# Four-layer convolution block, last image: the variance of the residual sum from a covariance, and the residual sums inside the q, k, v loop

## The chip, the cores and the metric

The kernel runs on one core of a Trainium2 chip, in float32. The metric is the device time of one execution in microseconds (us). Before the change it is 3103.75 us, the median of 3 runs (3103.21 to 3104.64). Stretches of the profile are given in us from the start of its span.

The engines: TensorE (PE; weight loads PEld) for matrix products, VectorE (DVE), ScalarE (ACT), GpSimd (POOL), and SyncE (SP), which issues most of the DMA transfers. Each runs its own instructions in their written order.

## The reference, cut to what matters

Four images of 256 channels and 64 x 64 pixels pass through four residual layers. Layer 0 is a convolution with group norm and a non-local attention over the 4096 pixels, layer 1 a linear attention, layer 2 a convolution with generated kernels, layer 3 a mixture of experts. Ahead of each layer stands a group norm. The change lies between layer 0 and layer 1:

```python
    # layer 0, its end
    attn = jax.nn.softmax(f, axis=-1)
    y = jnp.einsum('bnm,bmc->bnc', attn, g_x)
    ...
    w_y = group_norm(conv1x1(y, w_w, w_b), gn2_w, gn2_b)
    return w_y * 0.1 + xs
    ...
    x = x + _L0_conv_ref(_gn(x), ...)
    x = x + _L1_conv_ref(_gn(x), ...)    # layer 1: rmsnorm, q, k, v, context, out, rmsnorm
```

So layer 1 needs the group mean and variance of r + s * wy, where r is the residual (x plus the convolution's result, kept in `xs_d`), wy the attention's output after its 1 x 1 convolution, and s a scale per channel which is known only when the statistics of wy over the whole image are.

## The kernel before

The 256 channels are two halves (`h`) of 128 partitions; 4096 pixels are eight blocks (`q` or `c`) of 512 columns. The order of instructions on every engine is the order in which the Python code emits them. `Chain` (L47) is a generator with a rate, so that the tail of one image can be emitted in between the attention of the next.

**Attention.** `attend(b)` (L888) has eight blocks `q` of 16 iterations `m`. An iteration emits the logits of the next step (two products `pf`, two exponentials into a probability tile `pr`), four products `py`, and one addition into `tot` on VectorE. After each block, `ended` (L902) runs in four steps, one in each of the following iterations: sum `inv`, product `pss`, reciprocal, `yt`, the products `ps_wy` into `wt`, then `bn_stats` of `wt`, and the store of `wt` to `wy_d`. The wide working tiles (`pr`, `tot`, `wt`, `xg`, `sq`, `qk`, `v1`, `dw`, `wy`, ...) come from one pool, `k4` (L106), of nine buffers of 128 x 1024.

**Images.** While attention of image 3 (the last) runs, the tail of image 2 is emitted beside it (L1590). It ends with the load of the residual of image 3 into `x_cols` (L1546), and it leaves 16 products of its last layer in the list `held`. `fill(n)` puts n of these into places where TensorE would be idle, `settle` emits their additions (`res`) and stores. When the tail of image 2 is done, attention runs alone, and `residual_sums` (L956) is emitted beside it: 16 copies on ScalarE with an accumulator, for the mean of r.

**The tail of the last image.** `nonlocal_out` (L966) issues six loads of wy parts of 128 x 1024, waits for the end of the attention, and calls `group_finish` (L330) on the statistics of wy: aggregate, mean over a group by a product `pm`, variance by a product `pv`, `rstd` by a power on GpSimd (`rsqrt`, L215). `affine` gives scale `sc` and shift `sh`. Then come eight sums into `big` (for this image: `tpg`) of 128 x 1024 on VectorE (L1009, recorded as L127), each followed by a square with an accumulator on ScalarE (L1014); their total is the variance.

`linear_attention` (L1023) calls `group_finish` again, on that mean and variance. The loop over eight blocks `c` follows: `normed` (L1029) makes `xg` and its square `sq` on ScalarE and adds the halves into `s2` on VectorE; `qkv` (L1049) multiplies by `wqkv_s` (16 matmuls, `ps_qkv`), with the row norms by `norms` (L1040: product `ps_ss`, `rinv` on VectorE, a power on GpSimd), the exponentials of q and k (L1061) and the copy of v (L1062) on ScalarE; `context` (L1072) transposes q and accumulates the context. `normed(c + 1)` is emitted ahead of `qkv(c)`. For the last image the working tiles alternate between `k4` and four spare buffers (`in_turns`, L1561).

Of the kernel before, what the change touches and what calls it, by code (L numbers as in the profile page):

```python
# [93 lines left out]
def conv_preact_fast(ctx: ExitStack, tc: tile.TileContext, guard, x, wc, wtpg, ww, wqkv, wout, w1cat, wd2,  # L94
# [235 lines left out]
    def group_finish(st, avg, eps, shift=None):  # L330


        if callable(st):
            mv = st()
        else:
            mv = sp.tile([P, NH, 2], F32, name="mv")
            for h in range(NH):
                nc.vector.bn_aggr(mv[:, h, :], st[:, h, :, :].rearrange("p c s -> p (c s)"))
        if shift is not None:
            tt(mv[:, :, 0], mv[:, :, 0], shift, ALU.add)  # L340
        yield 1
        pm = bank("pm")
        nc.tensor.matmul(pm[:, 0:NH], avg, mv[:, :, 0], start=True, stop=True)
        gm = sp.tile([P, NH], F32, name="gm")
        nc.vector.tensor_copy(gm, pm[:, 0:NH])
        ev = sp.tile([P, NH], F32, name="ev")
        tt(ev, mv[:, :, 0], gm, ALU.subtract)
        tt(ev, ev, ev, ALU.mult)
        tt(ev, ev, mv[:, :, 1], ALU.add)
        yield 1  # L350
        pv = bank("pv")
        nc.tensor.matmul(pv[:, 0:NH], avg, ev, start=True, stop=True)
        rstd = sp.tile([P, NH], F32, name="rstd")
        nc.vector.tensor_scalar(rstd, pv[:, 0:NH], eps, None, ALU.add)  # L354
        rsqrt(rstd, rstd)
        return mv, gm, rstd
# [530 lines left out]

    def attend(b):  # L888

        probs, todo = {}, []  # L890
        st = wy_stats[b] = sp.tile([P, NH, 8, 6], F32, name="wy_st")

        def logits(i):
            q, m = divmod(i, NM)
            pr = k4("pr")
            for s in range(2):
                pf = bank("pf")
                nc.tensor.matmul(pf, phi[:, bass.ts(2 * m + s, P)], theta[:, bass.ts(q, 512)], start=True, stop=True)  # L898
                nc.scalar.activation(pr[:, bass.ts(s, 512)], pf, AF.Exp)  # L899
            probs[i] = pr  # L900

        def ended(q, py, tot):  # L902

            at = b * NQ + q
            inv = wk.tile([P, 512], F32, tag="inv", name="inv")
            nc.vector.scalar_tensor_tensor(inv, tot[:, 0:512], 1.0, tot[:, 512:CH], ALU.mult, ALU.add,
                                           accum_out=guard[:, 0, at:at + 1])
            yield
            pss = bank("pss")
            nc.tensor.matmul(pss, ones, inv, start=True, stop=True)  # L910
            yield
            nc.vector.reciprocal(inv, pss)  # L912
            yt = k2("yt")
            tt(yt, py, inv, ALU.mult)
            yield
            nc.scalar.activation(junk(), inv, AF.Copy, accum_out=guard[:, 1, at:at + 1])

            wt = k4("wt").rearrange("p (h n) -> p h n", h=NH)
            for h in range(NH):
                ps = bank("ps_wy")  # L920
                nc.tensor.matmul(ps, ww_s[:, bass.ts(h, P)], yt, start=True, stop=True)  # L921
                nc.scalar.copy(wt[:, h, :], ps)
            yield
            for h in range(NH):
                nc.vector.bn_stats(st[:, h, q, :], wt[:, h, :])
            nc.sync.dma_start(out=wy_d[b].rearrange("h p n -> p h n")[:, :, bass.ts(q, 512)], in_=wt)

        logits(0)
        for i in range(NQ * NM):
            q, m = divmod(i, NM)  # L930
            if m == 0:
                py = bank("py")
                tot = k4("tot")
            if i + 1 < NQ * NM:
                logits(i + 1)
            for s in range(2):
                nc.tensor.matmul(py, g[:, bass.ts(2 * m + s, P)], probs[i][:, bass.ts(s, 512)],  # L937
                                 start=(m == 0 and s == 0), stop=(m == NM - 1 and s == 1))
            if m == 1:
                tt(tot, probs[i - 1], probs[i], ALU.add)  # L940
            elif m > 1:
                tt(tot, tot, probs[i], ALU.add)
            for t in todo:
                next(t, None)
            if m == NM - 1:
                todo = [ended(q, py, tot)]
                next(todo[0])
            yield i + 1 < NQ * NM
        for t in todo:
            for _ in t:  # L950
                yield


    res_sum = cp.tile([P, NH], F32, name="res_sum")

    def residual_sums(xs_in):  # L956

        parts = sp.tile([P, NH, N // 512], F32, name="res_parts", bufs=1)
        for h in range(NH):
            for c in range(N // 512):  # L960
                nc.scalar.activation(junk(), xs_in[:, h, bass.ts(c, 512)], AF.Copy, accum_out=parts[:, h, c:c + 1])
                yield
        nc.vector.tensor_reduce(res_sum, parts, AX.X, ALU.add)


    def nonlocal_out(w, b, big, k4, xs_in):  # L966
# [4 lines left out]
        def load_parts(i):  # L971
            c, h = PARTS[i]
            wy = k4("wy")
# [7 lines left out]
        ahead = 2 if xs_in is None else 6  # L981
        parts = [load_parts(i) for i in range(ahead)]
        if xs_in is not None:
            yield 1
        bias = vec_s[:, V_WB, :]
        wmv, gm, rstd = yield from group_finish(wy_stats[b], avg32, 1e-5, bias)
        sc, sh = affine(gm, rstd, vec_s[:, V_G2W, :], vec_s[:, V_G2B, :], bias, 0.1)
        st = stats_tile()
        if xs_in is not None:

            mv = sp.tile([P, NH, 2], F32, name="mv_in", bufs=1)
            centre = sp.tile([P, NH], F32, name="centre", bufs=1)
            squares = sp.tile([P, NH, N // CH], F32, name="squares", bufs=1)
            tt(mv[:, :, 0], wmv[:, :, 0], bias, ALU.subtract)
            tt(mv[:, :, 0], mv[:, :, 0], sc, ALU.mult)
            stt(mv[:, :, 0], res_sum, 1.0 / N, mv[:, :, 0], ALU.mult, ALU.add)
            nc.vector.tensor_scalar(centre, mv[:, :, 0], -1.0, None, ALU.mult)

            def moments():
                nc.vector.tensor_reduce(mv[:, :, 1], squares, AX.X, ALU.add)  # L1000
                nc.vector.tensor_scalar(mv[:, :, 1], mv[:, :, 1], 1.0 / N, None, ALU.mult)
                return mv

            st = moments
        w.fill(2)
        for i, (c, h) in enumerate(PARTS):
            cols = bass.ts(c, CH)
            wy, xs = parts[i]
            stt(big[:, h, cols], wy, sc[:, h:h + 1], xs, ALU.mult, ALU.add)  # L1009
            if i + ahead < len(PARTS):  # L1010
                parts.append(load_parts(i + ahead))
            yield 0.6
            if xs_in is not None:
                nc.scalar.activation(wy, big[:, h, cols], AF.Square, bias=centre[:, h:h + 1], accum_out=squares[:, h, c:c + 1])  # L1014
            else:
                for s in range(2):
                    nc.vector.bn_stats(st[:, h, 2 * c + s, :], big[:, h, bass.ts(2 * c + s, 512)])
            yield 0.6
        w.settle()
        return st, sh  # L1020


    def linear_attention(w, b, big, qT, k4, st, sh, alone):  # L1023
        _, gm, rstd = yield from group_finish(st, avg8, 1e-5, sh)
# [56 lines left out]

        ahead = normed(0)
        yield 1
        ready = *ahead, None
        last = None
        for c in range(NC):
            if c + 1 < NC:
                ahead = normed(c + 1)
            yield 0.5
# [9 lines left out]
        rk = sp.tile([P, 1], F32, name="rk")  # L1099
# [98 lines left out]
    def generated(w, b, big, k4, st, sh, diag):  # L1198
        mv, gm, rstd = yield from group_finish(st, avg8, 1e-5, sh)

        pivot = sp.tile([P, NH], F32, name="pivot")
# [7 lines left out]
        hs = sp.tile([HT * HP, NC3], F32, name="hs")  # L1209
# [6 lines left out]
        b1n = sp.tile([HT * HP, 1], F32, name="b1n")  # L1216
# [33 lines left out]
        pooled = sp.tile([HT * HP, 1], F32, name="pooled")  # L1250
        nc.vector.tensor_reduce(pooled, hs, AX.X, ALU.add)
        pd = sp.tile([HT * HP, 2 * R], F32, name="pd")
# [5 lines left out]
        pb = sp.tile([P, 2 * R], F32, name="pb")  # L1258
# [3 lines left out]
        dk = sp.tile([P, NH * 9], F32, name="dk")  # L1262
# [177 lines left out]
    def mixed(w, b, big, k4, st, sh, held):  # L1440
# [7 lines left out]
        pool = sp.tile([P, NH], F32, name="rpool")  # L1448
# [6 lines left out]
        hid = sp.tile([EH, 1], F32, name="hid")  # L1455
# [6 lines left out]
        nm = sp.tile([P, 1], F32, name="lnm")  # L1462
        nc.vector.tensor_reduce(nm, pl[:, 0:NE], AX.X, ALU.max, negate=True)
        al = sp.tile([P, NE], F32, name="al")
        asum = sp.tile([P, 1], F32, name="asum")
# [5 lines left out]
        scales = sp.tile([P, NH, NE], F32, name="scales")  # L1471
# [15 lines left out]
        b3 = sp.tile([P, NH], F32, name="b3")  # L1487
# [46 lines left out]
    def tail(b, big, qT, k4=k4, diag=None, xs_in=None, held=None):  # L1534

        def layers(w):
            st, sh = yield from nonlocal_out(w, b, big, k4, xs_in)
            st = yield from linear_attention(w, b, big, qT, k4, st, sh, diag is not None)
# [33 lines left out]
    with tc.manual_schedule(engines={E.PE, E.Activation, E.DVE, E.Pool, E.SP}):  # L1572
# [20 lines left out]
        sums = residual_sums(x_cols)  # L1593
        while next(attention, False):
            for _ in range(3):
                next(sums, None)
        for _ in sums:
            pass
# [592 lines left out]
```

## Time and profile before

| what | us |
|---|---|
| median of 3 runs | 3103.75 |
| the profiled execution itself | 3104.24 |
| its span, first to last instruction | 3102.5 |
| attention of the last image, with the tail of image 2 beside it | about 2244 to 2820 |
| end of attention to the first `xg` of the last image's q, k, v loop | 2820.7 to 2848.73 |
| q, k, v loop of the last image, to the last context product | 2849.59 to 2914.5 |
| end of the span | 3102.5 |
| DMA: one load of 512 KB from `wy_d`, median from issue to landing | 4.7 |
| DMA: one load of 512 KB from `xs_d`, the same | 5.4 |

How to read it: a row of the timeline is start, duration, engine, line, operation, output and inputs; in brackets the idle time of its engine ahead of it, and what ended that. Many operations are issued by helpers, so L124 is any `tensor_tensor`, L127 any `scalar_tensor_tensor`, and L217 any power on GpSimd; the tile's name tells which. An accumulating operation is recorded as two, the second (`READ_ACCUMULATOR`) reading the accumulator. The chain of waits is followed back from the last instruction; what released a step is inferred. The granted clock is TensorE's, as a share of full speed. An operation's record is a little longer than its pitch: the eight sums take 1.28 us each, and start 1.195 us apart.

### The profile page before, as it was taken

To read this page: it belongs to the slowest core of one execution; us is meant where nothing else is said; L and a number is where in the kernel's file an instruction comes from. 1 tells how busy PE (TensorE), PEld (TensorE's weight loads), DVE (VectorE), ACT (ScalarE), POOL (GpSimd) and SP (SyncE) were. 2 spreads that over 40 slices of the span, in tenths; PEclk is the share of its full clock that TensorE was granted. 3 is DMA by queue.
4 is the path that set the end of the run, shared out by engine and by line. 5 is a ranking of instruction groups with operands and counts; after the bars stand their busy time and mean duration, and the time that the engine had idled before them with its cause. 6 is when DMAs were issued, how large, how long until landed. Compare 5 with 4: busy or idle time off the path is not lost.

```text
span 3102.5 us, 24417 instructions
## 1 busy us (share of the span) xinstructions
PE 3005.3 (97%) x8606; PEld 1486.3 (48%) x8606; DVE 2108.8 (68%) x2713; ACT 1173.3 (38%) x2188; POOL 131.0 (4%) x178
## 2 busy tenths in 40 slices
PE   6899999999999999999999999999999999998998
PEld 3354555445554444444565444444546544444643
DVE  8747777853557986787536897778363668865485
ACT  2134333353555332323364532222445443335621
POOL 0100000000010000000011000000000100000100
PEclk9999999999999999999999999999999999998999
DMA  5233111122100023113300102311420010021021
GB/s 218 79 100 140 34 48 31 34 51 79 51 11 30 12 75 126 38 38 65 115 8 4 34 27 75 115 41 34 95 82 1 11 34 7 16 80 68 8 68 66
DMA packets 58913, 174.25 MB, mean 56 GB/s; under 512 B 6432, under 2 KB 16416, under 8 KB 54560
## 3 DMA queue, kind: packets, MB, share of 16 engines
q1 hardware_dynamic: 54752, 155.85, 14.6%
q0 software_dynamic: 4032, 16.78, 2.9%
q8 instruction: 70, 1.15, 0.2%
q14 instruction: 59, 0.48, 0.1%
HBM read 111.26 MB, written 78.12 MB: 61 GB/s over the span
## 4 chain that ended last, share of the span: by engine, by line
PE 77%; DVE 16%; issue 5%; ACT 1%; DMA 0%; POOL 0%; POOLq 0%; ACTq 0%; DVEq 0%; SPq 0%
PE pf L898 22%; PE py L937 22%; PE ps_qkv L1057 5%; PE ps_conv L499 4%; PE ps_tp L874 4%; DVE dw L127 4%; PE ps_ex L1498 3%; DVE tot L124 3%; PE ps_pw L1298 3%; PE ps_conv L571 2%; PE ps_g L879 2%; PE ps_wy L921 2%; PE ps_o L1125 1%; PE ps_dw L1343 1%; DVE big L127 1%
## 5 line engine op out<-in xcount | busy, mean ns | idle before, releaser
L899 ACT ACTIVATE pr<-pf 128x512 f32<-128x512 f32 x1024 | 603.1, 596 | 1184.5 <-PE pf L898 1138.8
L898 PE MATMUL pf<-tpg 128*128 128x512 f32 x2048 | 969.3, 596 | 2.9 <-ACT pr L899 2.9
L937 PE MATMUL py<-pr,tpg 128*128 128x512 f32 x2048 | 962.3, 592 | 2.5 <-ACT pr L899 2.3
L124 DVE TENSOR_TENSOR tot<-tot,pr 128x1024 f32<-128x1024 f32 x448 | 546.0, 1219 | 181.1 <-ACT pr L899 179.7
L937 PEld LDWEIGHTS py<-pr,tpg 128*128 128x128 f32 x2048 | 388.8, 190 | 494.8 <-issue 476.1
L898 PEld LDWEIGHTS pf<-tpg 128*128 128x128 f32 x2048 | 381.9, 190 | 438.1 <-issue 412.5
L127 DVE SCALAR_TENSOR_TENSOR dw<-xp,dk,dw 128x1008 f32<-128x1008 f32 x208 | 262.9, 1267 | 9.9 <-ACT dw L1290 7.0
L499 PE MATMUL ps_conv<-v,u 128*128 128x512 f32 x384 | 171.0, 593 | 3.6 <-DVE v L124 3.6
L1057 PE MATMUL ps_qkv<-wqkv_s,xg 128*128 128x384 f32 x384 | 129.9, 487 | 0.0
L124 DVE TENSOR_TENSOR tpg<-ps_g,bg_s 128x512 f32<-128x512 f32 x32 | 22.1, 691 | 145.7 <-PE ps_g L879 145.7
L874 PE MATMUL ps_tp<-big,wtpg_s 128*128 128x512 f32 x256 | 118.1, 605 | 3.0 <-ACT big L671 3.0
L499 PEld LDWEIGHTS ps_conv<-v,u 128*128 128x128 f32 x384 | 72.6, 190 | 96.4 <-issue 89.8
L217 POOL TENSOR_TENSOR rstd<-rstd,half 128x2 f32<-128x2 f32 x24 | 16.8, 699 | 2359.6 <-DVE rstd L354 2227.4
L912 DVE RECIPROCAL inv<-pss 128x512 f32<-128x512 f32 x32 | 107.2, 3351 | 7.1 <-PE pss L910 7.1
L1298 PE MATMUL ps_pw<-dw,pk 128*128 128x512 f32 x224 | 101.3, 592 | 0.0
L1057 PEld LDWEIGHTS ps_qkv<-wqkv_s,xg 128*128 128x128 f32 x384 | 72.2, 190 | 53.5 <-issue 9.3
L1067 DVE TENSOR_REDUCE qs<-qk 128x16 f32<-128x512 f32 x24 | 16.5, 686 | 118.6 <-ACT qk L1061 118.6
L875 ACT ACTIVATE tpg<-ps_tp,btp_s 128x512 f32<-128x512 f32 x64 | 43.8, 686 | 119.7 <-PE ps_tp L874 119.7
L874 PEld LDWEIGHTS ps_tp<-big,wtpg_s 128*128 128x128 f32 x256 | 47.9, 195 | 55.0 <-issue 50.6
L1127 ACT ACTIVATE junk<-ps_o 128x256 f32<-128x256 f32 x128 | 49.1, 384 | 63.7 <-PE ps_o L1125 59.4
L1061 ACT ACTIVATE qk<-ps_qkv,rinv 128x256 f32<-128x256 f32 x96 | 45.5, 473 | 72.5 <-PE ps_qkv L1057 61.8
L124 DVE TENSOR_TENSOR v<-ra 128x1024 f32<-128x1024 f32 x58 | 69.5, 1219 | 0.4
(338 smaller groups left out, 3123.8 us busy)
## 6 DMA issues: line engine op xcount, KB each, us to landing
xp<-in_x_dram SPq DMA_DIRECT2D x16, 1024.0 KB, 6.5
wy_d<-wt SPq DMA_DIRECT2D x32, 512.0 KB, 3.0
out_dram<-res SPq DMA_DIRECT2D x64, 256.0 KB, 2.0
wy<-wy_d SPq DMA_DIRECT2D x28, 512.0 KB, 4.7
xs_d<-big POOLq DMA_DIRECT2D x24, 512.0 KB, 11.1
u<-filters SPq DMA_DIRECT2D x48, 256.0 KB, 2.5
xs<-xs_d SPq DMA_DIRECT2D x24, 512.0 KB, 5.4
u<-rows_d SPq DMA_DIRECT2D x36, 256.0 KB, 3.1
```

The source lines that it names most:

```text
L124: nc.vector.tensor_tensor(o, a, b, op)
L127: nc.vector.scalar_tensor_tensor(o, a, s, b, op0, op1)
L499: nc.tensor.matmul(ps[oh], u(oh, h), v[:, bass.ts(h, 512)], start=(h == 0), stop=(h == NH - 1))
L571: nc.tensor.matmul(ps[:, bass.ts(oh, IY * IX)], u[i][:, h, bass.ts(oh, P)], v[:, i, bass.ts(h, IY * IX)], start=(h == 0), stop=(h == NH - 1))
L874: nc.tensor.matmul(ps, wtpg_s[:, h, k, :], big[:, h, cols], start=(h == 0), stop=(h == NH - 1))
L898: nc.tensor.matmul(pf, phi[:, bass.ts(2 * m + s, P)], theta[:, bass.ts(q, 512)], start=True, stop=True)
L899: nc.scalar.activation(pr[:, bass.ts(s, 512)], pf, AF.Exp)
L912: nc.vector.reciprocal(inv, pss)
L937: nc.tensor.matmul(py, g[:, bass.ts(2 * m + s, P)], probs[i][:, bass.ts(s, 512)], start=(m == 0 and s == 0), stop=(m == NM - 1 and s == 1))
L1057: nc.tensor.matmul(ps[:, 0:3 * HID], xg[:, h, bass.ts(j, P)], wqkv_s[:, h, :], start=(h == 0), stop=(h == NH - 1))
L1298: nc.tensor.matmul(ps, pk[:, h * NH * P + oh * P:h * NH * P + (oh + 1) * P], dw[h][:, bass.ts(s, 512)], start=(h == 0), stop=(h == NH - 1))
L1498: nc.tensor.matmul(ps, wm[h][:, bass.ts(oh, P)], big[:, h, bass.ts(c, 512)], start=(h == 0), stop=(h == NH - 1))
```

## The change

It concerns the last image alone (and some small tiles, which now have one buffer in place of two).

1. In the last attention, a tile `xc` of `k4` is loaded from `xs_d` in every block, at m = 9: the block of r that belongs to the block of wy. At m = 12 and 14, `bn_stats` of its halves go to `res_st`. When the block's `wt` is there, `with_residual` multiplies (wy - pivot) by r with an accumulator (`joint`), one instruction for each half. The pivot is the mean of wy over the first block. The two multiplies of the last block are kept in `last_block`, and are emitted inside the first `group_finish` of the tail.
2. `residual_sums` and the squares are gone. Mean and variance of the sum follow from those of r and wy and from the covariance, by small operations of 128 x 2.
3. The eight sums are emitted by a generator, `on_the_way`: the first half-chunk of both halves inside the second `group_finish`, the rest inside the q, k, v loop, about a chunk ahead of `normed`.
4. The tail's wy parts come from `k4` alone, four loads ahead and two more at a time in the loop; before it were six, alternating between `k4` and the spare buffers.
5. One of the two held products filled in ahead of the sums is now filled in after the second `group_finish`; their additions are emitted there too, ahead of the loop.

```diff
-    def group_finish(st, avg, eps, shift=None):
+    def group_finish(st, avg, eps, shift=None, between=()):
...
         tt(ev, ev, mv[:, :, 1], ALU.add)
+        for f in between[0:1]:
+            f()
         yield 1
...
         rsqrt(rstd, rstd)
+        for f in between[1:]:
+            f()
...
+        def multiply(q, h, wt, xc):
+            nc.vector.scalar_tensor_tensor(xc[:, h, :], wt[:, h, :], pivot_in[:, h:h + 1], xc[:, h, :], ALU.add, ALU.mult,
+                                           accum_out=joint[:, h, q:q + 1])
+
+        def with_residual(q, wt, xc):
+
+            if q == 0:
+                mv = sp.tile([P, NH, 2], F32, name="mv")
+                for h in range(NH):
+                    nc.vector.bn_aggr(mv[:, h, :], st[:, h, 0, :])
+                nc.vector.tensor_scalar(pivot_in, mv[:, :, 0], -1.0, None, ALU.mult)
+            if q < NQ - 1:
+                for h in range(NH):
+                    multiply(q, h, wt, xc)
+            else:
+                last_block.extend(lambda h=h: multiply(q, h, wt, xc) for h in range(NH))
...
+            if b == B - 1:
+                with_residual(q, wt, xc)
...
+            if b == B - 1 and m == 9:
+                xc = k4("xc").rearrange("p (h n) -> p h n", h=NH)
+                nc.sync.dma_start(out=xc, in_=xs_d[b].rearrange("h p n -> p h n")[:, :, bass.ts(q, 512)])
+            if b == B - 1 and m in (12, 14):
+                h = m // 2 - 6
+                nc.vector.bn_stats(res_st[:, h, q, :], xc[:, h, :])
...
-            wy = k4("wy")
+            wy = (k4 if xs_in is None else pool4)("wy")
...
-        ahead = 2 if xs_in is None else 6
-        parts = [load_parts(i) for i in range(ahead)]
+        parts = [load_parts(i) for i in range(2 if xs_in is None else 4)]
...
+            tt(mv[:, :, 0], wmv[:, :, 0], bias, ALU.subtract)
+            tt(off, mv[:, :, 0], pivot_in, ALU.add)
+            for h in range(NH):
+                nc.vector.bn_aggr(rmv[:, h, :], res_st[:, h, :, :].rearrange("p c s -> p (c s)"))
+            nc.vector.tensor_reduce(cov, joint, AX.X, ALU.add)
+            tt(off, off, rmv[:, :, 0], ALU.mult)
+            stt(cov, cov, 1.0 / N, off, ALU.mult, ALU.subtract)
         sc, sh = affine(gm, rstd, vec_s[:, V_G2W, :], vec_s[:, V_G2B, :], bias, 0.1)
...
+            w.fill(1)
             tt(mv[:, :, 0], mv[:, :, 0], sc, ALU.mult)
...
+            tt(mv[:, :, 0], mv[:, :, 0], rmv[:, :, 0], ALU.add)
+            tt(mv[:, :, 1], wmv[:, :, 1], sc, ALU.mult)
+            stt(mv[:, :, 1], cov, 2.0, mv[:, :, 1], ALU.mult, ALU.add)
+            tt(mv[:, :, 1], mv[:, :, 1], sc, ALU.mult)
+            tt(mv[:, :, 1], mv[:, :, 1], rmv[:, :, 1], ALU.add)
+
+            def on_the_way():
+
+
+                for s in range(2):
+                    for h in range(NH):
+                        cols = bass.ts(s, 512)
+                        wy, xs = parts[h]
+                        stt(big[:, h, cols], wy[:, cols], sc[:, h:h + 1], xs[:, cols], ALU.mult, ALU.add)
+                        if s == 0:
+                            yield
+                yield
+                for c in range(1, N // CH):
+                    if c > 1:
+                        parts.extend(load_parts(2 * c + h) for h in range(NH))
+                        yield
+                    for h in range(NH):
+                        added(2 * c + h, sc)
+                    yield
+
+            return (lambda: mv), sh, on_the_way()
...
+        _, gm, rstd = yield from group_finish(st, avg8, 1e-5, sh, (lambda: next(sums),) * 2 if alone else ())
         nb = norm_bias(gm, rstd, sh)
...
+        if alone:
+            w.fill(1)
+        w.settle()
         ahead = normed(0)
+        if alone:
+            next(sums)
         yield 1
...
                 ahead = normed(c + 1)
+            if alone:
+                next(sums, None)
             yield 0.5
             this = yield from qkv(*ready)
```

## The prediction, made before the changed kernel was run

> **What bounds the kernel now.** I read the page first: one engine carries the span, and the clock falls at one place only.
>
> ```profile
> PE 3005.3 (97%) x8606; PEld 1486.3 (48%) x8606; DVE 2108.8 (68%) x2713; ACT 1173.3 (38%) x2188; POOL 131.0 (4%) x178
> ...
> PE   6899999999999999999999999999999999998998
> ...
> PEclk9999999999999999999999999999999999998999
> ```
>
> TensorE is full except at the start and in slice 37 (2792 to 2870 us), where the granted clock dips too. That slice holds the hand-over from the last attention to the tail of the last image. Next, the chain of work that ended last, for 2740 to 3103:
>
> ```profile
> 2828.41 2.75 DMA wy_d<-wt
> 2831.22 3.90 DMA rt<-wy_d
> 2835.15 8.45 DVE tpg L127 x7
> 2843.60 1.32 DVE res L127 x2
> 2845.39 0.60 PE pm L343 x2
> ...
> 2847.77 0.68 POOL rstd L217
> 2848.47 0.17 DVE nb L124
> 2848.73 0.82 ACT ra L1033
> 2849.59 2.93 PE ps_qkv L1057 x4
> 2852.52 1.50 PE ps_ss L1043 x8
> 2854.02 6.51 PE ps_qkv L1057 x12
> 2860.53 0.79 PE ps_ss L1043 x8
> 2861.32 5.27 PE ps_qkv L1057 x16
> ```
>
> The two DMA lines are an inference: the transfer happened to land at 2835.12, just as the second residual sum started behind the first. What holds the tail is the eight sums on VectorE with the squares on ScalarE behind them: the group statistics cannot start before all eight. From the third `ev` of the first statistics (end 2831.02) to the first `xg` (2848.73) it is 17.7 us, and TensorE has 0.7 us or less in each 2 us window between 2836 and 2848. Third, the windows, 2 us each (after the range: the length, then PE, PEld, DVE, ACT, POOL, and the granted clock):
>
> ```profile
> 2838.00:2840.00 2.00, 0.00 (x0) 0.00 (x0) 2.00 (x3) 2.00 (x4) 0.00 (x0) 1.00 0.00 0
> 2842.00:2844.00 2.00, 0.00 (x0) 0.00 (x0) 2.00 (x3) 2.00 (x5) 0.00 (x0) 0.50 0.00 0
> 2856.00:2858.00 2.00, 2.00 (x5) 1.09 (x4) 0.00 (x0) 1.21 (x4) 0.00 (x0) 0.50 0.00 0
> ```
>
> The clock halves in the gap and stays halved until about 2859, so the first chunk of q, k, v costs 11.73 us from 2849.59 to 2861.32, where a later chunk has 5.16 + 0.79 = 5.95. From 2868.76 each chunk is 7.34 us of TensorE without a gap.
>
> Call T the start of the first `xg` on ScalarE. Before: T = 2848.73, and the third chunk's products start at 2868.76 = T + 20.03. The path through the change is these two lengths.
>
> **Part 1, the statistics.** Removed from the path: eight sums at 1.195 us pitch (2833.95 to 2843.5), the last square (to 2844.9), two `res` additions standing between, two small operations. In their place, from 2831.02:
> - First `multiply` of the last block, between `ev` and `rstd`. Nearest row: the accumulating sum at L906, 0.69 us, next instruction 0.74 after its start. The matrix product it hides behind allowed `rstd` at 2831.50; now 2831.80, +0.3.
> - Second `multiply`, 0.74: to about 2832.6. Before, the power was done and `sc` started at 2832.56, so this costs nearly nothing.
> - Covariance: two aggregates at 0.31 and five small operations, dependent ones 0.19 apart: 1.3, to 2833.9. All of it stands ahead of `sc` in VectorE's order.
> - `affine`, six operations as now, 0.73 (2832.56 to 2833.29): to 2834.65.
> - Variance by formula, six operations and the shift, about 1.05: the shift starts at 2835.7.
> - From the shift to the first `xg` it was 2845.18 to 2848.73, 3.55. The first half-chunk sum (0.61) now stands between `ev` and `rstd`, where 0.84 passes anyway waiting for the product `pv`: nothing. The second stands beside the power on GpSimd.
>
> Here a rule speaks against the change. The trace has GpSimd powers beside a VectorE addition with both inputs in SBUF:
>
> ```profile
> 2432.21 0.17 DVE L1132 TENSOR_SCALAR zr<-zr 128x4 f32<-128x4 f32 x1 [1.81 <-ACT junk L1127]
> 2432.28 1.22 DVE L124 TENSOR_TENSOR tot<-tot,pr 128x1024 f32<-128x1024 f32 x1
> 2432.46 1.91 POOL L217 TENSOR_TENSOR zr<-zr,half 128x4 f32<-128x4 f32 x1 [8.50 <-DVE zr L1132]
> ```
>
> 1.91 us, where the median of this power is 1.008. The Trainium skill, "SBUF — State Buffer", section "Who interferes with whom", explains it: such a VectorE instruction and a GpSimd instruction that reads SBUF exclude each other for the whole instruction. The change puts one beside both `rstd` powers. The first is covered by covariance work. For the second: the sum ends 0.73 after `rstd` starts, the power needs about 0.55 more, 1.28 in place of the 1.03 measured (2847.44 to 2848.47): +0.25. Without the rule 0. I take 0.25, as the row agrees.
>
> So T after = 2835.7 + 3.55 + 0.25 = 2839.5, a gain of 9.2 (bounds 8.4 and 9.7, from a fifth either way on the roughly 3 us of small operations, and from the lock).
>
> **Part 2, the sums inside the q, k, v loop.** They don't vanish: 9.6 us of VectorE now run in the loop. After T: `s2` of chunk 0 comes at T + 2.64, as before (two `xg`, then the square), and ends T + 3.33. Its two remaining half-chunk sums end T + 4.6. ScalarE's `xg` of chunk 1 waits for them: T + 4.1 to 5.6, square to T + 6.7, `s2` to T + 7.4. Then two full sums, 2.4, to T + 9.8. Only behind them in VectorE's order stands the `rinv` of chunk 0; the exponentials wait for it: from `rinv` to `exp` is 1.28 (2854.47 to 2855.75), so T + 11.1, where it was T + 7.02. That is 4.1 late, and it is what is late next. Following on: four exponential pairs 2.6, `xg` and square of chunk 2 2.6, `s2` 0.7 (T + 17.0), norms 0.8, transposes and context 1.4: the third chunk starts at T + 19.3, against T + 20.03 now. The delay is absorbed because before, TensorE at half clock took those 19 us itself. It has done chunk 1 by about T + 16, or T + 17.9 if the clock stays halved until T + 9, which makes T + 20.1. Bounds: T + 18.5 and T + 21.5; I take 19.3, gain 0.7.
>
> A rule on the clock bears on that. The rows show half clock up to 9 us after the products began. The Trainium skill, "TensorE: Matmul & The Clock Gate", "Part 1: The HAM clock gate", has full clock after about 3.4 us of sustained work. One held product (four matmuls) is moved to stand just ahead of the loop, so by the rule full clock comes near T + 2 to T + 5; by the rows, which I follow for the bound, near T + 8. The sum is 19.3 by the one and 20.1 by the other. The product itself delays the first q, k, v product by 0.9 at half clock, covered by the wait for `s2`.
>
> From the third chunk on, ScalarE has about 6 of 7.34 us to do and VectorE 2.5, plus 2.4 in every second chunk: covered by TensorE, 0. Uncovered it would be 2.4 a time. Loads 4 to 7 are issued one chunk (7.3 us) ahead, against 4.7 to land: 0.
>
> **Part 3, the last attention.** Added: eight loads of 512 KB on SyncE's queue, 16 statistics at 0.61 pitch, 14 multiplies at 0.74, three small operations: 21 us of VectorE between 2244 and 2820. VectorE is idle for about 205 of the 580 us from 2240 to 2820, and TensorE waits for nothing there: the list of TensorE's waits is empty. It is tightest here:
>
> ```profile
> 2540.00:2560.00 20.00, 20.00 (x48) 8.89 (x47) 19.82 (x20) 6.68 (x12) 0.00 (x0) 1.00 0.18 52
> ```
>
> A lump of 1.3 us lands in it. What TensorE needs from VectorE then, `inv`, ends at 2560.6 and `pss` starts 2565.9: 5.3 spare. The pointwise products at 2592.5 follow the last tap by 1.9, and VectorE idles 0.8 and 0.9 shortly before. Queued behind a statistic that waits for its load are the `tot` additions, which free the probability buffers. The load has three iterations of 3.43 = 10.3 us against 5.4 to land (the page's `xs` loads). On SyncE the store of `wt` and the tail's loads queue behind it, as they now do behind stores.
>
> The unknown is the buffer: `xc` holds one of nine of `k4` for 10 of 16 iterations. The trace doesn't show how many are spare. No gain is possible, TensorE having no gap; removing 16 ScalarE copies with their accumulator reads (12.3 us) gains nothing for the same reason. Upper end: one exponential, 0.6, uncovered in each of some 37 holding iterations of the tap stage: 22. Nearest row: TensorE's empty wait list. I take 0.5. The `bufs=1` edits cost nothing: their tiles are used once an image.
>
> **Sum.** Against the profiled execution's own time, 3104.24 (span 3102.5 and 1.74 around it): 3104.24 - 9.2 - 0.7 + 0.5 = 3094.84. The median of the runs is 0.49 below that execution, so 3094.4.
>
> **Rivals.** (a) The loop gives it back: the exponentials' 4.1 us are not absorbed, because TensorE would have been warm anyway. 3103.75 - 9.2 + 4.1 + 0.5 = 3099.2. For it: `rinv` stands behind two full sums. Against: the 11.73 us of the first chunk. (b) Slower: `xc` starves the probability ring. At 22 us, 3103.75 - 9.9 + 22 = 3115.9; it decides above 9.9 / 37 = 0.27 us per holding iteration. For it: nine buffers shared by attention, taps and filters, with VectorE at 19.8 of 20. Against: VectorE catches up within 15 us, and TensorE never waited. (c) The change doesn't free the path because the first sums wait for reloads: all four early loads now take `k4` buffers. Three such loads were issued by 2805.3; even one issued at 2820 lands by 2825, twelve us before need. A late one costs 2 to 5: 3096 to 3099.
>
> **Chances.** Forecast 0.74; (a) 0.12; (b) 0.07, most of it slower; (c) 0.07. Measurement tells about 0.2% (6.2 us) from no change, so faster means below 3097.5. Of (c), and of milder forms of (a), a little counts as faster: 0.79 faster, 0.15 within, 0.06 slower. Range 3091.0, by the good ends of parts 1 and 2, to 3100.0, which takes in (a).
>
> **What would show it.** Right: in the changed trace no squares at L1014; the first `xg` 8.4 to 9.7 us earlier after the attention's last `inv`; the first exponential about 11 after `xg`; the third chunk about 19 after it; both `rstd` powers above 0.70; the attention's length unchanged within 1 us. Wrong: TensorE waits before 2820, or the third chunk beyond T + 21.5.

## The result and the profile after

The changed kernel takes 3094.76 us (median of 9 runs, 3093.55 to 3097.48) against 3103.75: ratio 0.9972, 95% interval 0.9963 to 0.9981. The forecast was 3094.4. Its profiled execution spans 3093.0 us, 9.5 less than the 3102.5 before. The number is close; the terms behind it are less so: one part came out 3.2 us worse than forecast, and what made up for it, 3.3 us in all, was in good part luck.

The page of the changed kernel, the same lines as before:

```profile
PE 3002.1 (97%) x8606; PEld 1485.2 (48%) x8606; DVE 2130.3 (69%) x2772; ACT 1153.3 (37%) x2140; POOL 131.8 (4%) x178
...
PE   6899999999999999999999999999999999998998
...
PEclk9999999999999999999999999999999999999999
```

VectorE has 21.5 us more to do, ScalarE 20 us less, TensorE the same matmuls: the gain is no saved work. The chain of waits, from the second statistics into the loop:

```profile
2836.45 0.16 DVE ev L124
2836.61 0.51 DVE tpg L127
2837.13 0.07 issue
2837.19 0.16 DVE rstd L357
...
2837.52 1.05 POOL rstd L217
...
2838.79 1.53 ACT ra L1088 x2
...
2846.15 2.39 DVE tpg L127 x2
2848.54 0.08 DVE rinv L1100
...
2854.85 0.70 DVE s L124
2855.55 0.14 issue
2855.69 1.84 PE ps_ss L1098 x8
2857.52 0.95 PE ps_qt L1131 x4
2858.48 1.72 PE ps_ctx L1134 x8
2860.20 6.35 PE ps_qkv L1112 x16
2866.55 0.79 PE ps_ss L1098 x8
```

The eight sums and the two DMA lines are gone from in front of the first `xg` (here `ra L1088`, 2838.79). Two sums (2846.15) now stand in the chain ahead of `rinv`. The last lines hold what the forecast lacked: the norms `ps_ss` take 1.84 and then, four lines on, 0.79 for the same eight matmuls. The windows (columns as in the prediction) show why, and a row of the timeline has the wait ahead of it:

```profile
2854.00:2856.00 2.00, 0.31 (x2) 0.34 (x2) 0.69 (x1) 1.82 (x5) 1.01 (x2) 0.91 0.00 0
2856.00:2858.00 2.00, 2.00 (x11) 2.00 (x11) 0.63 (x1) 1.59 (x6) 0.00 (x0) 0.50 0.62 152
2862.00:2864.00 2.00, 2.00 (x7) 1.20 (x6) 2.00 (x3) 0.73 (x2) 0.00 (x0) 0.88 0.00 0
```

```profile
2855.69 1.84 PE L1098 MATMUL ps_ss<-ones,s 128*128 128x1 f32 x8 [2.43 <-DVE s L124]
```

TensorE had finished the second chunk (`c` = 1) at 2853.26 and waited 2.43 us for the third chunk's `s2`; then its clock was halved until 2862.5.

The table gives the stages of every profiled run, counted from the start of the attention's last product `pss`, since the attention itself ends up to 1.5 us earlier or later from run to run (`pss` starts between 2819.87 and 2821.40). T is the first `xg`; the first exponential is counted from T; then the products of the third and fourth chunk, the first `ps_dw` of the layer after, and the end of the span.

| run | T | first exp | third chunk | fourth chunk | `ps_dw` | end | median us |
|---|---|---|---|---|---|---|---|
| before | 28.15 | T + 7.02 | 48.02 | 55.36 | 157.66 | 281.92 | 3103.75 |
| the change | 18.15 | T + 10.94 | 39.35 | 47.92 | 148.53 | 272.36 | 3094.76 |
| e1 attention part only | 28.15 | T + 7.02 | 48.09 | 55.43 | 157.75 | 282.10 | 3104.26 |
| e2 sums ahead of the loop | 18.58 | T + 15.00 | 46.85 | 54.19 | 156.52 | 280.76 | 3101.66 |
| e3 product in the gap | 18.14 | T + 10.95 | 39.64 | 46.98 | 147.76 | 271.83 | 3094.74 |
| e4 rinv first | 18.15 | T + 9.52 | 35.88 | 43.22 | 144.22 | 268.33 | 3091.08 |
| e5 norms ahead | 18.59 | T + 7.85 | 38.06 | 45.40 | 146.29 | 270.63 | 3093.48 |
| e6 no sums in the loop | 18.59 | T + 8.56 | 35.36 | 42.70 | 143.33 | 267.39 | 3089.62 |
| e7 as e4, sum behind nb | 18.21 | T + 9.81 | 36.23 | 43.57 | 145.92 | 270.51 | 3092.01 |
| e8 the change again | 18.16 | T + 10.95 | 39.37 | 47.82 | 150.17 | 275.13 | 3096.28 |
| e9 sums in one block | 18.59 | T + 9.52 | 38.44 | 46.88 | 149.20 | 274.27 | 3096.55 |
| e10 e4 again | 18.58 | T + 9.52 | 36.31 | 43.65 | 145.95 | 270.54 | 3091.16 |

So between the first two rows: 10.0 us gained at T, 7.44 left at the fourth chunk, 9.13 at `ps_dw`, 9.56 at the end. TensorE's work behind the fourth chunk's start is the same in all twelve profiles, and took between 224.4 us (the change) and 227.4 (e9); the kernel before has 226.6.

With the short statistics T is about 18.15 or about 18.59 (e7, of which below, apart). The difference is the clock: in every profile it is halved at the end of the attention (at 2831.7 in the change), for 3.41 us in the change, e3, e4 and e8, and for 10.24 us in e2, e5, e6, e7, e9 and e10. There the two products of the second statistics take 0.59 us each in place of 0.38. TensorE's work is the same up to that point, and e4 and e10 are one program throughout, so which of the two it is comes by chance.

### The profile page after: what moved, and what is told of

It is laid out like the page before. It is cut to its first block, busy times and chain, and to the rows that moved or that the text cites. A ratio compares the mean times of both kernels' runs of the same rounds, so it can differ in the third digit from the quotient of the medians.

```text
span 3093.0 us, 24447 instructions
## 1 busy us (share of the span) xinstructions
PE 3002.1 (97%) x8606; PEld 1485.2 (48%) x8606; DVE 2130.3 (69%) x2772; ACT 1153.3 (37%) x2140; POOL 131.8 (4%) x178
## 4 chain that ended last, share of the span: by engine, by line
PE 77%; DVE 16%; issue 5%; ACT 2%; POOL 0%; DMA 0%; POOLq 0%; DVEq 0%; ACTq 0%
PE pf L926 22%; PE py L968 22%; PE ps_qkv L1112 5%; PE ps_conv L504 4%; PE ps_tp L879 4%; DVE dw L127 4%; PE ps_ex L1560 3%; DVE tot L124 3%; PE ps_pw L1360 3%; PE ps_conv L576 2%; PE ps_g L884 2%; PE ps_wy L949 2%; PE ps_o L1187 1%; PE ps_dw L1405 1%; DVE big L127 1%
```

## The experiments

The theory: the gain is the statistics' path, which no longer holds the eight sums; the loop gives part of it back, through `rinv` behind two sums and the clock dip that follows; the attention's extra work is free; and the 2.1 us gained behind the fourth chunk are the clock's chance, not the change's. The rivals: the attention's part costs time which a larger gain hides; the gain is the overlap of the sums with the loop; the gain behind the loop belongs to the change.

**e1, the attention's part alone.** The changed kernel with `nonlocal_out`, `linear_attention` and `residual_sums` as they were.

> The attention's part alone: loads of the residual block, its statistics and the multiplies by it (all but the two of the last block) are done, but nothing uses them; mean and variance come from the residual sums and the squares as before. Theory (the gain is the shorter statistics path, and the attention's extra work lies under TensorE): the time of the kernel before within 1 us, 3102.8 to 3104.8, and the list of TensorE's waits in the attention stays empty. Rival (the buffer held by the residual block, or VectorE's extra 21 us, costs TensorE time, so that the tail gains more than the whole shows): 3106 or more, with waits of TensorE before 2820.

Measured 3104.26, ratio 1.0002 (0.9993 to 1.001), and TensorE has no wait in the attention. Every stage of the table, all of them behind the attention, repeats the kernel before within 0.2 us. The attention itself ended 0.8 us later (`pss` at 2821.40 against 2820.58), inside the spread from run to run; in the change it ended 0.06 later. So neither VectorE's added work (2128.1 us against 2108.8) nor the buffer held made TensorE wait, and no cost shows above the noise, which is some 2 to 3 us either way. The rival falls.

**e2, the sums ahead of the loop.**

```diff
+        if alone:
+            for _ in sums:
+                pass
         ahead = normed(0)
-        if alone:
-            next(sums)
...
-        parts = [load_parts(i) for i in range(2 if xs_in is None else 4)]
+        parts = [load_parts(i) for i in range(2 if xs_in is None else 6)]
...
-                    if c > 1:
+                    if c > 2:
```

> Covariance statistics as in the change, but the six later sums and the two second half-chunk sums stand ahead of the q, k, v loop in one block, not in it. T, the first xg, stays about 2838.8. Theory (what counts is that the statistics no longer wait for the sums; where the sums stand matters little, because the first exponentials wait for VectorE either way): the sum of the halves of chunk 0 comes at about T + 9.6 in place of T + 2.6, the first exponential at T + 12.8 in place of T + 10.9, the third chunk 1.5 to 3 us later than in the change, 3096 to 3098.5 in all. Rival (the gain is the overlap of the sums with the loop): all of the 7.2 us come back, 3101 to 3103.

Measured 3101.66, ratio 0.9993 (0.9985 to 1.0001): the rival's number, and not mine. T is 0.4 us late, by the clock, and otherwise where it should be; 1.2 us of the gain at T are left at the fourth chunk. So the short statistics alone give almost nothing. Two rows of its timeline:

```profile
2841.19 8.58 DVE L127 SCALAR_TENSOR_TENSOR tpg<-wy,sc,xp 128x512 f32<-128x512 f32 x8
2850.43 1.87 PE L1098 MATMUL ps_ss<-ones,s 128*128 128x1 f32 x8 [8.65 <-DVE s L124]
```

The eight sums start 2.5 us late (behind a `res` that waits for the held product), `s2` queues behind them, and TensorE, with no more to do than four matmuls, sits idle 8.65 us and runs the first chunk at half clock again (granted clock 0.50 from 2848 to 2856). I had priced the delay of the first exponential (T + 12.8; it was T + 15.0) and had left out what the idle time does to the clock. The longer half clock at the attention's end adds over 1 us to the held product here (3.66 us against 1.96), but luck with the clock doesn't save the theory: the fastest of 13 runs took 3100.45.

**e3, the product in the gap.**

```diff
-        if alone:
-            w.fill(1)
         w.settle()
         ahead = normed(0)
...
             this = yield from qkv(*ready)
+            if alone and c == 1:
+                w.fill(1)
             if c + 1 < NC:
                 ready = *ahead, norms(ahead[1])
+            w.settle()
```

> The change, with the second held product moved from ahead of the loop into the gap of TensorE after the second chunk (where it waits 2.4 us for s2 of the third). Theory (that wait halves the clock, and the halved clock costs 3.5 us between 2855.7 and 2866.6: norms 1.05, transposes and context 1.25, products 1.2): the granted clock stays at 1.00 there, the fourth chunk starts 2.5 to 3.5 us earlier, 3091 to 3092.5 in all. Rival (the clock falls for the low load of the whole stretch, not for this wait): the dip stays, and the time is that of the change or 1 us above, 3094 to 3096.

Measured 3094.74, ratio 0.997 (0.9959 to 0.9981): the time of the change. Both expectations were half right. The dip of the third chunk is gone, as the theory had it; but another has come in its place, at the start:

```profile
2840.38 2.93 PE ps_qkv L1112 x4
2843.31 1.50 PE ps_ss L1098 x8
2844.80 6.42 PE ps_qkv L1112 x12
...
2857.28 1.72 PE ps_ex L1561 x4
2859.00 0.79 PE ps_ss L1098 x8
```

Its timeline has the wait that is new:

```profile
2840.38 2.93 PE L1112 MATMUL ps_qkv<-wqkv_s,ra 128*128 128x384 f32 x4 [2.60 <-ACT ra L1088]
```

The granted clock is 0.50 from 2839.4 to 2849.6. The first chunk's twelve matmuls take 6.42 us here, as in the kernel before (6.51); in the change, where the product stood just ahead of the loop, 4.12 by the timeline. In these two profiles the held product kept the clock up at whichever place it stood.

**e4, rinv first.**

```diff
-            if alone:
+            if alone and c > 0:
                 next(sums, None)
...
                 if rinv is None:
                     rinv = norms(s2)
+                    if alone:
+                        next(sums)
```

> The change, with rinv of the first chunk emitted ahead of the two full sums that stand before it on VectorE. rinv moves from T + 9.7 to T + 7.4. Theory (the sums ahead of rinv set the first exponential): it comes earlier, at T + 9.7 if GpSimd's power gets in between the two sums, and the third chunk with it, by up to 1.2 us; with less waiting the clock may stay up: 3091 to 3094. Rival (the power is locked out until both sums are done): the first exponential stays at T + 10.9, and the time at 3094 to 3096.

Measured 3091.08, ratio 0.9959 (0.9945 to 0.9972): the theory. Only the order of one tiny instruction and two sums is changed. In the change `rinv` had started at 2848.46, behind both sums, 5.2 us after its input was done. The timeline of e4:

```profile
2846.80 0.15 DVE L1100 TENSOR_SCALAR rinv<-ps_ss 128x4 f32<-128x4 f32 x1
2846.87 2.47 DVE L127 SCALAR_TENSOR_TENSOR tpg<-wy,sc,xp 128x1024 f32<-128x1024 f32 x2
2847.03 1.98 POOL L217 TENSOR_TENSOR rinv<-rinv,half 128x4 f32<-128x4 f32 x1 [7.68 <-DVE rinv L1100]
...
2855.00 1.02 PE L1098 MATMUL ps_ss<-ones,s 128*128 128x1 f32 x8 [1.01 <-DVE s L124]
```

The power takes 1.98 in place of 1.01: it is locked out by the first sum, and gets in before the second has ended. The exponential comes 1.4 us sooner, the third chunk 3.5 us sooner: the rest is the clock, which stays at 1.00 through the whole loop, now that TensorE's wait has shrunk to 1.01 us. The same wait in e7 and e10 left the clock at 1.00 too.

**e5, the norms ahead of the loop.**

```diff
-        ready = *ahead, None
+        ready = *ahead, norms(ahead[1]) if alone else None
```

(moved up, to stand right behind `normed(0)`)

> The change, with the row norms of the first chunk (products ps_ss, rinv, power) emitted ahead of the loop, so before the chunk's own products and before all full sums. Theory (what is late is rinv of the first chunk behind the sums, and the clock that falls in the wait this makes): the first exponential waits only for ScalarE's own order, T + 7.3 in place of T + 10.9, the third chunk at T + 17 to T + 18, 3090 to 3091.5 in all. Rival (the clock decides: TensorE now waits for the norms with nothing to do, and starts the first chunk at half clock): third chunk at T + 20 or later, 3093 to 3095.

Measured 3093.48, ratio 0.9968 (0.9956 to 0.9981). The first exponential came early (T + 7.85), but the third chunk at T + 19.5, between the two expectations: TensorE's first chunk starts only after the norms, and partly at half clock (0.65 from 2844 to 2848), so that it takes 7.75 us to the second chunk where 5.95 is the length at full clock. The time is the rival's.

**e6, no sums in the loop.** `on_the_way` without its two lines `added(2 * c + h, sc)`.

> The change with the six full sums of the loop left out (the loads stay), so that 6 of 8 parts of the layer's input are not what they should be: it prices the sums in the loop. Theory (they cost by standing ahead of the first rinv and by the clock dip that follows, not by their 7.2 us): the third chunk at T + 17 to T + 18, as with rinv first, 3090 to 3091.5. Rival (the sums cost VectorE time all through the loop): 3087 to 3089.

Measured 3089.62, ratio 0.9958 (0.9944 to 0.9971). The time lies between the two expectations. The third chunk is at T + 16.8, 0.2 below the range that the theory gave. Counted from T, which is 0.44 later here than in the change and e4, the fourth chunk comes 5.7 us sooner than in the change, and 1.0 sooner than in e4 and e10. So six sums, 7.2 us of VectorE, cost 5.7 us as the change has them, and 1.0 with `rinv` first.

**e7, as e4, with the second half-chunk sum behind nb.**

```diff
-(lambda: next(sums),) * 2 if alone else ()
+(lambda: next(sums),) if alone else ()
...
         nb = norm_bias(gm, rstd, sh)
+        if alone:
+            next(sums)
```

> rinv of the first chunk ahead of its two full sums, as in the run before, and the second half-chunk sum emitted behind nb in place of beside the power on GpSimd. Theory (a VectorE sum with two inputs in SBUF locks the power out: 1.05 us in the change, 0.69 before it): the power takes 0.70 again, and T comes 0.35 us sooner after the attention's last product pss (17.65 in place of 18.0); in all 0 to 0.5 us under the run before. Rival (the power is long for another reason): it stays at 1.05.

The power beside the sum, in the change, and without it, here:

```profile
2837.49 1.07 POOL L217 TENSOR_TENSOR rstd<-rstd,half 128x2 f32<-128x2 f32 x1 [4.45 <-DVE rstd L357]
```

```profile
2838.37 0.70 POOL L217 TENSOR_TENSOR rstd<-rstd,half 128x2 f32<-128x2 f32 x1 [4.77 <-DVE nb L124]
```

The power took 0.70, and from `rstd` to `nb` it was 1.03 us in place of 1.39 in e4. But T did not come sooner than in e4 (18.21 against 18.15), since in this profile the two statistics products ran at half clock, 0.59 each in place of 0.38. Beside the profiles with the same half clock there (e5, e6, e9 and e10, T 18.59), it came 0.37 sooner: that is what the sum beside the power costs. At the third chunk 0.1 of it is left against e10, and the time, 3092.01 (ratio 0.9961, 0.9948 to 0.9975), can't be told from e4.

**e8, the change again.**

> The changed kernel once more, unaltered, for a second profile and more times. Theory (2.1 of the 9.5 us between the two profiles come from where the granted clock dips behind the loop, not from an instruction of the change): the loop repeats (T 18.0 and the fourth chunk 47.9 after pss, within 0.3, if the clock does the same there), while the stretch from the fourth chunk to the end varies by 1 to 3 us with the clock. Rival (the later gain belongs to the change): the stretch is the same within 0.3 us.

Measured 3096.28, ratio 0.9973 (0.9962 to 0.9984). Up to the fourth chunk the second profile repeats the first within 0.1 us; behind it, it loses 2.9. The rows are of the same matmuls, in the change and in its repetition:

```profile
2956.73 5.32 PE L1294 MATMUL ps_h<-tpg,w1n 128*32 128x512 f32 x31
```

```profile
2957.01 7.01 PE L1294 MATMUL ps_h<-tpg,w1n 128*32 128x512 f32 x31
```

The second row has a stretch of half clock in it, 2958.2 to 2961.6, which the first has not. 7.01 is also what the kernel before has, with half clock from 2964.8 to 2968.2. So of the 9.56 us between the first two profiles 2.1 were a lucky clock behind the loop; the change's own gain is 7.4 to the fourth chunk, and its medians lie 7.4 and 9.0 below those of the kernel before.

**e9, all sums in one block behind rinv.** As e4, with `for _ in sums: pass` in place of `next(sums)` behind the norms, and six loads ahead.

> rinv of the first chunk ahead of the full sums, and all six of them in one block right behind it, instead of two at a time; six loads ahead in place of four. Theory (sums ahead of the loop cost 7 us because s2 and rinv of the first chunk queue behind them and TensorE goes idle and to half clock, not because they are together): with the first chunk's s2 and rinv ahead of the block, the third chunk starts within 1.5 us of the run with rinv first (35.9 after pss), 3090.5 to 3093. Rival (VectorE's sums must be spread over the loop): the block delays the first chunk's q scaling and the third chunk's s2, TensorE waits, and 4 to 7 us come back, 3095 to 3098.

Measured 3096.55, ratio 0.9978 (0.997 to 0.9986): the rival. Three rows:

```profile
2846.26 7.25 DVE L127 SCALAR_TENSOR_TENSOR tpg<-wy,sc,xp 128x1024 f32<-128x1024 f32 x6
2846.43 1.98 POOL L217 TENSOR_TENSOR rinv<-rinv,half 128x4 f32<-128x4 f32 x1 [7.68 <-DVE rinv L1100]
2855.95 1.02 PE L1098 MATMUL ps_ss<-ones,s 128*128 128x1 f32 x8 [2.56 <-DVE s L124]
```

The block (7.25 us) delays the scaling of q and the third `s2` on VectorE; TensorE waits 2.56 us for it, its clock is halved once more (2857.6 to 2861.0), and the third chunk comes 2.1 us later than in e10, the fourth 3.2 us.

**e10, e4 again.**

> The run with rinv first once more, unaltered, for its times. If its gain over the change (3.7 us) is from the loop, it repeats: third chunk 35.9 after pss, 3090 to 3092.5. Rival (it was a good draw of the clock behind the loop): 3093 to 3096 with the same loop.

Measured 3091.16, ratio 0.996 (0.9946 to 0.9973). It repeats, though T came 0.4 us later and the part behind the loop was a worse draw. Ten runs of e4 and e10 lie from 3089.82 to 3092.73, sixteen of the change from 3093.46 to 3097.91: the order with `rinv` first beats both kernels: by some 12.5 us the kernel before, and by 3.7 to 5.2 us the change.

## Why the prediction was right, and where not

- **The bound** (eight sums hold the tail, the DMA lines a coincidence): right. Neither line is in the chain after. But e2 shows that it was half of the matter: shortening the statistics is worth 9.6 us at T and 1.2 us at the fourth chunk if the sums then stand ahead of `s2`. And the clock does not fall at one place only: the page's row has a second 8, in its last slice. In the kernel before it is 0.50 from 2951.2 to 2958.0, 2964.8 to 2968.2 and 3057.0 to 3063.8 too; the 2.1 us below come from the middle one, which the change's profile has not.
- **Part 1**, 9.2 forecast, bounds 8.4 to 9.7: measured 10.0, outside them. Each small term was a little too large: covariance 1.16 for 1.3, variance and shift 0.93 for 1.05, the first `multiply` 0.12 for 0.3; and the two statistics products ran at full clock, 0.38 for 0.59. That last 0.42 was luck: in six profiles with the same work of TensorE up to there they took 0.59. The lock was too small: the power took 1.07, which is 0.37 more, for 0.25.
- **Part 2**, 0.7 gain forecast at the third chunk: measured a loss of 1.3 (T + 21.2, where the table has T + 19.9 for before), and 1.2 more inside that chunk. The chain of VectorE and ScalarE was as worked out: exponential at T + 10.94 (11.1), `s2` of the third chunk with its norms at T + 16.9 (17.0). The step that failed is the one after it, "norms 0.8, transposes and context 1.4": they took 1.84 and 2.67, at half clock. The text had TensorE done with the second chunk by T + 16 and `s2` ready at T + 17.0, a wait of 1 us. But the clock was at 1.00 from 2835.2 on, before T, where the text had it rise near T + 2 to T + 5, or T + 8. So TensorE was done at T + 14.5, and waited 2.43 us. What a wait does to the clock was not in the sum: I used the clock rule for warming up, and not for falling. Rival (a), that the loop gives the gain back because TensorE is warm, was more than half true: the loop gave back 2.5 us of its 4.1. Its chance had been put at 0.12.
- **Part 3**, 0.5: nothing that can be told from zero. The attention ended 0.06 us later in the change's profile and 0.8 in that of e1, where it varies by 1.5 from run to run. Nothing of the 22 of rival (b) came. Of rival (c), nothing: the first sum starts as soon as `ev` is done, so its load had landed.
- **The sum** came out because part 2 with the chunk that follows it fell 3.2 short (0.7 to be gained, 2.5 lost), and this was met by 0.8 in part 1, 0.4 in part 3, and 2.1 from the clock behind the loop, which the prediction did not count and which e8 does not repeat. That the sum is right within 0.4 us is luck; that the statistics' path is worth 9.6 to 10.0 us at T is not.

## What to carry to other kernels

A statistic can be taken off the path by working it out from parts that are known earlier; but what is moved out of the way must also land where no small instruction of the critical chain queues behind it. Look on the in-order engine for the tiny instruction behind the big ones (`rinv` behind two sums): here its place was worth 3.7 to 5.2 us, about half of the whole change. And cost every new wait of TensorE twice: its length, and the half clock that a wait of 2.4 us brought to the next 6.8 us.

## What was not expected of the hardware

- A wait of TensorE of 2.43 us, inside a stretch that was otherwise full, halved the clock for 6.8 us (granted clock 1.00 to 2855.6, 0.50 to 2862.5); waits of 2.44 us in e8, 2.56 in e9, 2.60 in e3 and 1.61 in e5 went with a fall too, and waits of 1.01 in e4, e7 and e10 did not. The Trainium skill, "TensorE: Matmul & The Clock Gate", section "Part 1: The HAM clock gate", has an idle window of about 3.4 us for the fall; here TensorE had worked for 1.0 us of the 3.41 ahead of the fall, so it came sooner. In the kernel before, the half clock lasted 9 us into the products.
- The clock changes on a beat. Between its first and last change every stretch at one clock, in all twelve profiles, is a whole number of times 3.413 us long: half clock lasted 3.41 (e9), 6.83 (the change), 10.24 (e3) and 17.07 (the kernel before) in or ahead of the loop. So the time from the start of a wait to the fall differs: 2.4 us in the change, 4.2 in e9, 5.2 in the kernel before. And what a wait costs depends on where it lies on the beat: the same wait of 2.10 us at the attention's end was followed by 3.41 us of half clock where the fall came 11.1 us after the start of `pss` (the change), and by 10.24 where it came 9.9 us after (e10). How much of a beat must be idle stays open: in the beat ahead of its fall e9 has 1.8 us of idle time, and the kernel before has as much in one that no fall follows (2836.7 to 2838.5).
- GpSimd's power gets in between two VectorE sums that follow each other without a gap: 1.98 us beside six in a row (e9) as beside two (e4), which is the first sum and its own time. So the lock costs one sum and not the queue.
- The same program draws different clock dips: 5.32 or 7.01 us for the same 31 matmuls, and 2.9 us in all from the fourth chunk to the end. Differences of 1 to 2 us between single profiles of this kernel can't be read without the clock's row beside them.
